# A decoder kernel: queries and keys projected once and turned by a shuffle, the cross attentions' sums taken two units to a step, the other products in the steps between, in halves of one bank

## The chip, the cores and the metric

The kernel runs on one core of a Trainium2 chip. The profile names the core's engines PE (the matrix engine; PEld is its weight load), DVE (the vector engine), ACT (the scalar engine), POOL, and SP, which issues transfers. The metric is the device time of one launch in microseconds (us): before the change the median of three runs is 1469.78 us (1468.67 to 1469.87).

## What is computed

The input is 16 batches of 128 tokens with 256 channels. Two decoder layers follow each other, each with self attention, cross attention and a feed-forward part, a residual sum and a layer norm after each. The two cross attentions matter here. In layer 0, which projects and rotates its queries and keys, the reference says (cut):

```python
q = jnp.einsum('oi,bit->bot', wq, x) + bq[None, :, None]
k = jnp.einsum('oi,bit->bot', wk, c) + bk[None, :, None]
v = jnp.einsum('oi,bit->bot', wv, c) + bv[None, :, None]
...
q = apply_rope(q, ROPE_D)
k = apply_rope(k, ROPE_D)
scores = jnp.einsum('bhqc,bhkc->bhqk', q, k) / math.sqrt(K_CHANNELS)
...
p_attn = jax.nn.softmax(scores, axis=-1)
out = jnp.einsum('bhqk,bhkc->bhqc', p_attn, v)
...
out = jnp.einsum('oi,bit->bot', wo, out) + bo[None, :, None]
```

It has 16 heads of 8 channels. The rotation multiplies each of a head's first four channels by a cosine and adds, times a sine, the channel two places away. Layer 1's cross attention has 8 heads of 16 channels and no projections: its queries are the tokens, its keys and values both the context.

## The kernel before

**Beats.** Each attention is written as a pipeline in beats. `by_beats` (L274) gets blocks of (beats per batch, lag, scores, jobs, order of batches). In every beat it first calls the scores' `beat(s, t)`, then `sums` if any are due, then the jobs that are due. PE runs its products in exactly this order (`mm`, L238, and `turned`, L242, keep it), and the attention's DVE, ACT and POOL instructions are kept in program order too (`Written`, L190). So an instruction that waits holds up everything behind it on its engine.

**Scores.** A unit is what one beat handles: two heads of one chunk of 128 queries or keys. `cross_scores` (L428) does two things in one beat. For the unit `s` it makes scores in a tile `ps_st` (two PSUM banks), whose negated row maxima DVE takes with a TENSOR_REDUCE. For the unit `t`, which is `lag` beats older, it makes the transposed scores less the maxima in another `ps_st`, from which ACT's exponential writes `pT`. Both use products on a quarter of PE's rows, so they run side by side; in the trace they are the groups of form 32*128. Late in the pipeline three `ps_st` tiles go round, so the scores of one beat go where the exponential of the beat before has read.

**Sums.** `sums` (L472) multiplies the exponentials with the values, in products of form 128*32, into `ps_o` (one bank). It is due two beats after its unit's exponential: one unit in each beat. In layer 0 a unit takes 8 matmul instructions, in layer 1 it takes 16 (an f32 product is two instructions in the trace).

**Jobs.** All other products of the two cross attentions go into `ps_m`. After a `switch` in the course of each pipeline it is one bank with one buffer. Each job sits at a beat offset from its batch's first beat. In layer 0 (8 beats per batch, lag 11, L975) the jobs with PE products are `keys` (-10), `queries` (-5), `values` (5), `maxima` (9), `finish` (26), `gate_turn` (28), and for every second batch `gate` (32) and `places` (39). Taken modulo 8 these fall on eight different beats. `queries` and `keys` call `side` (L920): two projections of 256 columns into one bank, the second with the weights' rows swapped so that it holds the mate channels; `rotated` (L800) then does cosine times the first on DVE, a bias on the second on ACT, sine times it and the sum on POOL. In layer 1 (4 beats per batch, lag 6, L1380) the jobs with products are `values` (0), `cross_maxima` (5), `turn_block` (18), and for every second batch `route` (19), `score` (23 and 24).

**What follows a job.** Each product in `ps_m` is read by ACT or DVE: `values` by an ACT copy to `v`, `maxima` by an ACT copy to `nmT` that the next exponentials' products need, `gate_turn` by an ACT copy. In both layers `out` copies `ps_o` on ACT, `invert` takes a logarithm and an exponential of the sums on ACT (`ol`), and the layer norm's `rstd` is a POOL instruction between DVE instructions.

Layer 0's feed-forward part (eight experts) and layer 1's (dense, plus a lookup) lie outside the attention pipelines and have their own loops.

Of the kernel before, what the change touches and what calls it, by code (L numbers as in the profile page):

```python
# [18 lines left out]
P = 128  # L19
D = 256  # L20
# [11 lines left out]
def kernel(ctx: ExitStack, tc: tile.TileContext, a: dict, out: bass.AP):  # L32
# [121 lines left out]

    xw = load(cpool, [P, 8, P], a["xw"], "xw", eng=nc.gpsimd)
    xb = load(cpool, [P, 6], a["xb"], "xb", eng=nc.gpsimd)
    bv2 = load(cpool, [P, D], a["bv2"].partition_broadcast(P), "bv2", eng=nc.gpsimd)
# [87 lines left out]
    class InTurn:  # L245
# [5 lines left out]
        def tile(self, *args, **kw):  # L251
            self.n += 1
            return self.pools[self.n % len(self.pools)].tile(*args, **kw)

    def attention_tiles(st, ahead):
# [4 lines left out]
        single = st.enter_context(tc.tile_pool(name="ps_m", bufs=1, space=PSUM))  # L260
        extra = st.enter_context(ExitStack())
        more = extra.enter_context(tc.tile_pool(name="ps_m2", bufs=2, space=PSUM))
        pl = dict(st=scores, o=sums, m=InTurn(more, single, more))

        def switch():
            extra.close()
            pl["st"] = InTurn(scores, scores, extra.enter_context(tc.tile_pool(name="ps_st2", bufs=1, space=PSUM)))
            pl["m"] = single

        for name, bufs in (("w", 2), ("q", ahead), ("p", 4)):  # L270
            pl[name] = st.enter_context(tc.tile_pool(name=f"att_{name}", bufs=bufs))
        return pl, switch

    def by_beats(blocks, switch=None, at=None):  # L274
# [153 lines left out]
    def cross_scores(pl, heads, kept, lag):  # L428
# [68 lines left out]

        return dict(beat=beat, sums=sums)

# [406 lines left out]
    def rope_cross_plain(pl):  # L906
# [4 lines left out]
        def biases(b):  # L911

            if b:
                return
            pb = pl["m"].tile([P, 1], F32, name="ps_m")
            mm(pb, lhsT=xw[:, 5, :], rhs=xb[:, 5:6], start=True, stop=True)
            bias_of["ov"] = const.tile([P, 1], F32, name="bias_ov")
            vec.tensor_tensor(bias_of["ov"], pb, xb[:, 4:5], ALU.add)

        def side(b, n, src):  # L920
            pab = pl["m"].tile([P, 2, D], F32, name="ps_m")
            for i in range(2):
                mm(pab[:, i, :], lhsT=xw[:, 2 * n + i, :], rhs=src, start=True, stop=True)
            return rotated(pl, pab, n, "wq"[n])

        def queries(b):
            q = side(b, 0, x_t[b])
            z = pl["q"].tile([P, 4, D], F32, name="z")
            for i in range(4):
                pool.tensor_scalar_mul(z[:, i, :], q, hm[:, 2 + i : 3 + i])  # L930
            kept[b]["qz"] = z

        def keys(b):
            kept[b] = {}
            kept[b]["k"] = side(b, 1, ctx_t[b])

        def values(b):
            pv = pl["m"].tile([P, 2, P], F32, name="ps_m")
            for kc in range(2):
                mm(pv[:, kc, :], lhsT=ctx_t[b][:, kc * P : (kc + 1) * P], rhs=xw[:, 4, :], start=True, stop=True)  # L940
            v = kept[b]["v"] = v8[b % 2]
# [25 lines left out]
        def finish(b):  # L967
            oT = kept[b][1]
            kept[b] = cross_output(pl, b, bias_of["ov"], (6, oT[:, 0, :]), (7, oT[:, 1, :]))
# [12 lines left out]
        return 8, 11, cross_scores(pl, 16, kept, 11), jobs, range(B)  # L982

    def rope_cross_masked(st):
# [3 lines left out]
        for b in range(B):  # L988
            rot = []
            for n, src in ((0, x_t[b]), (1, ctx_t[b])):  # L990
                pab = pl["m"].tile([P, 2, D], F32, name="ps_m")
                nc.tensor.matmul(pab[:, 0, :], lhsT=xw[:, 2 * n, :], rhs=src, start=True, stop=True)
                nc.tensor.matmul(pab[:, 1, :], lhsT=xw[:, 2 * n + 1, :], rhs=src, start=True, stop=True)
                rot.append(rotated(pl, pab, n, "w"))
            z = pl["w"].tile([P, 4, D], F32, name="z")
# [3 lines left out]
            for kc in range(2):  # L999
                nc.tensor.matmul(  # L1000
                    pv[:, kc, :], lhsT=ctx_t[b][:, kc * P : (kc + 1) * P], rhs=xw[:, 4, :], start=True, stop=True
                )
# [4 lines left out]
            oT = cross_heads(pl, 16, rot[0], [z[:, i, :] for i in range(4)], v, dict(masked, v=vn))  # L1007
            xn, stats = cross_output(pl, b, xb[:, 4:5], (5, oT.rearrange("p c q -> p (c q)")))
            scaled(x_t[b], xn, stats)
# [178 lines left out]
    with ExitStack() as st:  # L1188
# [177 lines left out]
        def best(b):  # L1366
# [10 lines left out]
            for hf in range(2):  # L1377
# [234 lines left out]
def layouts(inputs):  # L1612
# [6 lines left out]

    mate = row + np.where(c < 2, 2, np.where(c < 4, -2, 0))  # L1620
    theta = np.float32(1.0) / np.float32(10000.0) ** (np.arange(0, 4, 2, dtype=np.float32) / np.float32(4))
# [13 lines left out]
    for n in range(2):  # L1635
# [10 lines left out]
        "w0": np.stack([i[f"L0_attn_w_{n}"].T for n in "qkvo"], 1),  # L1646
        "xw": np.stack([wq.T, wq[mate].T, wk.T, wk[mate].T, wv.T, wo.T] + pairs, 1),
        "xb": np.stack([bq, bq[mate], bk, bk[mate], bo, i["L0_xattn_bv"]], 1),
        "bv2": np.concatenate([i["L0_xattn_bv"]] * 2),
# [43 lines left out]
```

## Time and profile before

| What | Value |
|---|---|
| Median of the runs | 1469.78 us |
| The profiled execution's own time | 1472.02 us |
| Its span, from first to last instruction | 1470.3 us |
| Mean granted clock of PE | 0.959 |
| DVE busy | 810.8 us |
| ACT busy | 595.7 us |
| POOL busy | 289.6 us |
| DVE's row maxima (TENSOR_REDUCE on `ps_st`) | 256 of 1221 ns |
| ACT's exponentials (`pT`) | 224 of 1024 ns |

The stretches of the span, by the view of windows (busy us of each engine):

| Stretch (us) | Work | PE | DVE | ACT | clock |
|---|---|---|---|---|---|
| 35 to 200 | layer 0 self attention, cross attention filling | 151.42 | 148.53 | 75.37 | 0.99 |
| 200 to 500 | layer 0 cross attention | 298.76 | 228.00 | 173.37 | 0.99 |
| 500 to 860 | end of it, experts, start of layer 1 | 304.72 | 59.37 | 71.14 | 0.90 |
| 860 to 1020 | layer 1 self attention | 158.60 | 122.23 | 76.34 | 0.96 |
| 1020 to 1210 | layer 1 cross attention | 175.37 | 125.86 | 108.01 | 0.99 |
| 1210 to 1470 | layer 1 feed-forward | 237.88 | 104.69 | 88.00 | 0.96 |

A row of the timeline gives start, length, engine, line, operation, output<-inputs, shapes and how many were merged; in brackets stands how long the engine had been idle and what ended that. A line of the view of windows gives the stretch, its length, each engine's busy time with the count of instructions, and PEclk, the share of full speed that PE's clock was granted.

### The profile page before, as it was taken

What the parts mean: (1) busy time and instruction counts of PE and PEld (TensorE: products, weight loads), DVE (VectorE), ACT (ScalarE), POOL (GpSimd) and SP (SyncE); (2) the same over time, 40 slices, a digit from 0 to 9 for tenths busy, and PEclk for the clock granted to TensorE, in tenths of its full rate; (3) what the DMA queues carried; (4) which work ended last, traced back from release to release, by engine and by line L of the source; (5) the groups of instructions that cost most, each with busy time, mean ns of one, the idle gap of its engine ahead of it and who ended that gap; (6) DMA issues with size and microseconds to landing.
All of it is one profiled execution on the core that took longest, in us unless ns stands there. A gap on an engine that the chain in (4) does not pass through costs nothing. (4 is left out here: it accounts for less than half of the span.)

```text
span 1470.3 us, 28836 instructions
## 1 busy us (share of the span) xinstructions
PE 1338.7 (91%) x11993; PEld 857.1 (58%) x11993; DVE 810.8 (55%) x2085; ACT 595.7 (41%) x1051; POOL 289.6 (20%) x402
## 2 busy tenths in 40 slices
PE   3999999999999938999999589999999989989997
PEld 2656555555555415777888456665555544446666
DVE  6899876777777530100110168876767656543222
ACT  1454426555655611111112135543555556761110
POOL 7000243344444120000000233312121100000000
PEclk9999989999999968999999769999999998999999
DMA  9200000000000006222330411000000000000000
GB/s 300 68 2 2 2 1 2 2 16 16 16 12 12 23 28 193 96 94 92 112 129 15 158 37 31 23 2 1 2 1 2 2 2 1 0 2 15 15 8 22
DMA packets 42780, 57.15 MB, mean 39 GB/s; under 512 B 5929, under 2 KB 32569, under 8 KB 42633
## 3 DMA queue, kind: packets, MB, share of 16 engines
q1 hardware_dynamic: 37192, 41.99, 8.8%
q0 software_dynamic: 4608, 12.34, 2.6%
q8 instruction: 99, 1.62, 0.5%
q10 hardware_dynamic: 832, 0.80, 0.2%
q14 instruction: 49, 0.39, 0.1%
HBM read 38.73 MB, written 16.38 MB: 37 GB/s over the span
## 5 line engine op out<-in xcount | busy, mean ns | idle before, releaser
L199 DVE TENSOR_REDUCE nm<-ps_st 128x4 f32<-128x1024 f32 (+1 forms) x256 | 312.6, 1221 | 123.1 <-PE ps_st L240 119.7
L199 ACT ACTIVATE pT<-ps_st 128x1024 f32<-128x1024 f32 x224 | 229.4, 1024 | 197.3 <-PE ps_st L240 195.5
L199 POOL TENSOR_TENSOR rstd<-ve,nhalf 128x1 f32<-128x1 f32 x112 | 62.7, 561 | 752.1 <-DVE ve L199 630.9
L240 PE MATMUL ps_o<-pT,v 128*32 128x256 f32 (+1 forms) x2560 | 164.5, 347 | 0.5 <-DVE oT L199 0.4
L240 PE MATMUL ps_st<-rot,z 32*128 32x256 f32 x1024 | 147.8, 405 | 2.2 <-DVE nm L199 2.2
L1077 DVE TENSOR_TENSOR ye<-ps_e,b 128x256 f32<-128x256 f32 (+6 forms) x38 | 16.1, 424 | 238.7 <-PE ps_e L1074 238.7
L240 PE MATMUL ps_st<-z,rot 32*128 32x512 f32 x512 | 131.7, 592 | 0.0
L1066 ACT ACTIVATE h<-ps_h,b 128x672 f32<-128x672 f32 (+7 forms) x64 | 46.6, 728 | 204.3 <-PE ps_h L1062 192.3
L1062 PE MATMUL ps_h<-h,w 128*128 128x336 f32 (+7 forms) x512 | 122.1, 399 | 0.0
L1062 PEld LDWEIGHTS ps_h<-h,w 128*128 128x128 f32 x512 | 97.2, 190 | 23.6
L240 PEld LDWEIGHTS ps_o<-pT,v 128*32 128x32 f32 x2560 | 54.6, 108 | 96.2 <-issue 82.4
L240 PE MATMUL ps_st<-nmT,pick 32*128 32x256 bf16 x1024 | 100.7, 274 | 9.8 <-ACT nmT L199 7.4
L240 PEld LDWEIGHTS ps_st<-rot,z 32*128 32x128 f32 x1024 | 91.0, 187 | 14.5 <-issue 5.1
L199 POOL DMA_INDIRECT y<-ys,place x32 | 31.1, 973 | 284.6 <-DVE absT L1195 276.9
L240 PE MATMUL ps_o<-pT,ones 128*32 128x256 f32 x1024 | 79.2, 380 | 0.0
L240 PEld LDWEIGHTS <-pick 32*128 32x128 bf16 x1024 | 30.3, 92 | 79.1 <-issue 72.1
L240 PE MATMUL ps_st<-ctx,z 32*128 32x256 f32 x512 | 73.1, 403 | 0.0
L240 PE MATMUL ps_f<-fxT,fgw 128*128 128x512 f32 x128 | 62.4, 611 | 7.1 <-ACT g L1409 7.1
L1062 PE MATMUL ps_h<-xeT,w 128*128 128x336 f32 (+7 forms) x256 | 65.2, 414 | 4.0 <-DVE xeT L1054 2.1
L1074 PE MATMUL ps_e<-w,h 128*128 128x256 f32 (+6 forms) x304 | 67.3, 379 | 0.0
L240 PE MATMUL ps_st<-z,ctx 32*128 32x512 f32 x256 | 66.6, 596 | 0.0
L1074 PEld LDWEIGHTS ps_e<-w,h 128*128 128x128 f32 (+6 forms) x304 | 54.9, 181 | 11.0 <-issue 1.0
(295 smaller groups left out, 2356.2 us busy)
## 6 DMA issues: line engine op xcount, KB each, us to landing
w<-in_W_dram SPq DMA_DIRECT2D x16, 512.0 KB, 4.0
w<-in_W_dram SPq DMA_DIRECT2D x8, 1024.0 KB, 5.7
xs<-zero SPq DMA_DIRECT2D x42, 128.0 KB, 4.2
xe<-xs SPq DMA_DIRECT2D x32, 128.0 KB, 3.5
ys<-ye SPq DMA_DIRECT2D x32, 128.0 KB, 3.7
x<-in_x_dram SPq DMA_DIRECT2D x16, 128.0 KB, 7.4
ctx<-in_ctx_dram POOLq DMA_DIRECT2D x16, 128.0 KB, 5.9
out_dram<-x SPq DMA_DIRECT2D x16, 128.0 KB, 1.7
```

Source lines behind the costliest of these rows:

```text
L199: instruction = getattr(self.engine, name)(*args, **kw)
L240: tc.keep_in_program_order(nc.tensor.matmul(*args, **kw))
L1062: nc.tensor.matmul(ps[:, n, 0:H], lhsT=w[:, c, hc * P : (hc + 1) * P], rhs=src[:, c, n * H : (n + 1) * H], start=(c == 0), stop=(c == part ...
L1066: nc.scalar.activation(dst[:, hc, 0:cap].rearrange("p (n t) -> p n t", n=2), ps[:, :, 0:H], AF.Gelu, bias=b12[:, layer, hc : hc + 1],)
L1074: nc.tensor.matmul(ps[0:m], lhsT=h2[:, fc, c : c + m], rhs=w3[:, fc, :], start=(fc == 0), stop=(fc == 3))
L1077: nc.vector.tensor_add(ye[0:m, c // P, :], ps[0:m], b3[0:m])
```

## The change

**Sums in pairs.** `cross_scores` returns `pairs=True`, and `by_beats` puts an odd unit's sums one beat earlier, so that two units' sums stand in one beat and the next beat has none. This holds for both cross attentions.

**Jobs between.** The offsets of the jobs move so that those with PE products mostly fall on the beats without sums. Layer 0's lag becomes 12. Layer 0's PE jobs are now `keys` -11, `queries` -7, `values` 7, `maxima` 10, `finish` 27, `gate_turn` 29, `gate` 33, `places` 39. In layer 1 `values` is at -1, `turn_block` at 17; `cross_out`, `cross_invert` and `cross_add` are one beat earlier than before.

**One projection, and a shuffle.** `side` goes. `projected` makes one projection and ACT adds its bias (`plain`). A beat later `rotated` shuffles `plain` across partitions on DVE to get the mate channels and multiplies by the cosine on DVE; sine and sum stay on POOL. The swapped weights and biases leave the inputs. The masking of the queries by head (`one_head_left`, four POOL instructions) becomes a job of its own.

**Half banks.** After the switch `ps_m` is one tile of a whole bank, `ps_half`, and jobs take its two halves in turn (`Halves`). Before the switch the three banks that were two pools become one pool of three.

```diff
+    class Halves:
+        def __init__(self, bank):
+            self.bank, self.n = bank, 0
+
+        def tile(self, shape, dtype, name):
+            self.n += 1
+            half = self.bank[:, self.n % 2, :]
...
         def switch():
             extra.close()
             pl["st"] = InTurn(scores, scores, extra.enter_context(tc.tile_pool(name="ps_st2", bufs=1, space=PSUM)))
-            pl["m"] = single
+            last = extra.enter_context(tc.tile_pool(name="ps_m2", bufs=1, space=PSUM))
+            pl["m"] = Halves(last.tile([P, 2, D], F32, name="ps_half"))
...
-                    beats.setdefault(n + lag + 2, [[], [], []])[1].append((score["sums"], b, h))
+                    late = h % 2 if score.get("pairs") else 0
+                    beats.setdefault(n + lag + 2 - late, [[], [], []])[1].append((score["sums"], b, h))
...
-    def rotated(pl, pab, n, dst):
-
+    def biased(pl, ps, n):
+
+        t = pl["w"].tile([P, D], F32, name=f"plain{n}")
+        act.activation(t, ps, AF.Identity, bias=xb[:, n : n + 1])
+        return t
+
+    def rotated(pl, plain, n, dst):
+
+        t1 = pl["w"].tile([P, D], F32, name="rot_t")
+        vec.stream_shuffle(t1, plain, mates)
         t0 = pl[dst].tile([P, D], F32, name=f"rot{n}")
-        t1 = pl["w"].tile([P, D], F32, name="rot_t")
-        vec.scalar_tensor_tensor(t0, pab[:, 0, :], xb[:, 2 * n : 2 * n + 1], rope[:, 0, :], ALU.add, ALU.mult)
-        act.activation(t1, pab[:, 1, :], AF.Identity, bias=xb[:, 2 * n + 1 : 2 * n + 2])
+        vec.tensor_tensor(t0, plain, rope[:, 0, :], ALU.mult)
         pool.tensor_tensor(t1, t1, rope[:, 1, :], ALU.mult)
         pool.tensor_tensor(t0, t0, t1, ALU.add)
         return t0
...
-        def side(b, n, src):
-            pab = pl["m"].tile([P, 2, D], F32, name="ps_m")
-            for i in range(2):
-                mm(pab[:, i, :], lhsT=xw[:, 2 * n + i, :], rhs=src, start=True, stop=True)
-            return rotated(pl, pab, n, "wq"[n])
+        def projected(n, src):
+            pq = pl["m"].tile([P, D], F32, name="ps_m")
+            mm(pq, lhsT=xw[:, n, :], rhs=src, start=True, stop=True)
+            return biased(pl, pq, n)
...
-        jobs = [(8, parts), (9, maxima), (20, out), (21, spread), (22, invert), (25, divide), (-11, biases), (-10, keys),
-                (-5, queries), (5, values), (26, finish), (27, scale_rows)]
-        for beat, part in ((28, gate_turn), (32, gate), (33, gate_best), (35, gate_rows), (39, places)):
+        jobs = [(8, parts), (10, maxima), (20, out), (21, spread), (22, invert), (24, divide), (-12, biases), (-11, keys),
+                (-10, turn_keys), (-7, queries), (-6, turn_queries), (-5, one_head_left), (7, values), (27, finish),
+                (28, scale_rows)]
+        for beat, part in ((29, gate_turn), (33, gate), (34, gate_best), (36, gate_rows), (39, places)):
...
-        return 8, 11, cross_scores(pl, 16, kept, 11), jobs, range(B)
+        return 8, 12, cross_scores(pl, 16, kept, 12), jobs, range(B)
...
-            [(4, cross_parts), (5, cross_maxima), (11, cross_out), (12, cross_invert), (13, cross_add), (14, cross_scale),
-             (0, values), (-2, queries), (18, turn_block), (19, route), (23, lambda b: score(0, b)),
+            [(4, cross_parts), (5, cross_maxima), (10, cross_out), (11, cross_invert), (12, cross_add), (14, cross_scale),
+             (-1, values), (-2, queries), (17, turn_block), (19, route), (23, lambda b: score(0, b)),
```

More of the change, by code (lines that the diff above doesn't have):

```diff
@@ L152 @@
     nc.gpsimd.memset(zero, 0.0)
-    xw = load(cpool, [P, 8, P], a["xw"], "xw", eng=nc.gpsimd)
-    xb = load(cpool, [P, 6], a["xb"], "xb", eng=nc.gpsimd)
+    xw = load(cpool, [P, 6, P], a["xw"], "xw", eng=nc.gpsimd)
+    xb = load(cpool, [P, 4], a["xb"], "xb", eng=nc.gpsimd)
     bv2 = load(cpool, [P, D], a["bv2"].partition_broadcast(P), "bv2", eng=nc.gpsimd)
@@ L253, in tile @@
             return self.pools[self.n % len(self.pools)].tile(*args, **kw)
+    class Halves:
[4 more added lines that the diff above has]
+            half = self.bank[:, self.n % 2, :]
+            if dtype == BF16:
+                half = half.bitcast(BF16)
+            half = half[0 : shape[0], 0 : math.prod(shape[1:])]
+            return half if len(shape) == 2 else half.rearrange("p (a b) -> p a b", a=shape[1])
     def attention_tiles(st, ahead):
@@ L259, in attention_tiles @@
         sums = st.enter_context(tc.tile_pool(name="ps_o", bufs=1, space=PSUM))
-        single = st.enter_context(tc.tile_pool(name="ps_m", bufs=1, space=PSUM))
         extra = st.enter_context(ExitStack())
-        more = extra.enter_context(tc.tile_pool(name="ps_m2", bufs=2, space=PSUM))
-        pl = dict(st=scores, o=sums, m=InTurn(more, single, more))
+        pl = dict(st=scores, o=sums, m=extra.enter_context(tc.tile_pool(name="ps_m", bufs=3, space=PSUM)))
         def switch():
@@ L496, in sums @@
                 )
-        return dict(beat=beat, sums=sums)
+        return dict(beat=beat, sums=sums, pairs=True)
     def attention_pools(st):
@@ L797, in ternary @@
         return 2, 3, causal_scores(pl, kept, qk_scale), jobs, range(B)
-    def rotated(pl, pab, n, dst):
+    mates = [n + (2 if n % 8 < 2 else -2 if n % 8 < 4 else 0) for n in range(32)]
+    def biased(pl, ps, n):
[5 more added lines that the diff above has]
+        vec.stream_shuffle(t1, plain, mates)
         t0 = pl[dst].tile([P, D], F32, name=f"rot{n}")
-        t1 = pl["w"].tile([P, D], F32, name="rot_t")
-        vec.scalar_tensor_tensor(t0, pab[:, 0, :], xb[:, 2 * n : 2 * n + 1], rope[:, 0, :], ALU.add, ALU.mult)
-        act.activation(t1, pab[:, 1, :], AF.Identity, bias=xb[:, 2 * n + 1 : 2 * n + 2])
+        vec.tensor_tensor(t0, plain, rope[:, 0, :], ALU.mult)
         pool.tensor_tensor(t1, t1, rope[:, 1, :], ALU.mult)
@@ L915, in biases, with turn_queries, one_head_left, turn_keys @@
             pb = pl["m"].tile([P, 1], F32, name="ps_m")
-            mm(pb, lhsT=xw[:, 5, :], rhs=xb[:, 5:6], start=True, stop=True)
+            mm(pb, lhsT=xw[:, 3, :], rhs=xb[:, 3:4], start=True, stop=True)
             bias_of["ov"] = const.tile([P, 1], F32, name="bias_ov")
-            vec.tensor_tensor(bias_of["ov"], pb, xb[:, 4:5], ALU.add)
-        def side(b, n, src):
-            pab = pl["m"].tile([P, 2, D], F32, name="ps_m")
-            for i in range(2):
-                mm(pab[:, i, :], lhsT=xw[:, 2 * n + i, :], rhs=src, start=True, stop=True)
-            return rotated(pl, pab, n, "wq"[n])
+            vec.tensor_tensor(bias_of["ov"], pb, xb[:, 2:3], ALU.add)
+        def projected(n, src):
+            pq = pl["m"].tile([P, D], F32, name="ps_m")
+            mm(pq, lhsT=xw[:, n, :], rhs=src, start=True, stop=True)
+            return biased(pl, pq, n)
         def queries(b):
-            q = side(b, 0, x_t[b])
+            kept[b]["q"] = projected(0, x_t[b])
+        def turn_queries(b):
+            kept[b]["q"] = rotated(pl, kept[b]["q"], 0, "w")
+        def one_head_left(b):
             z = pl["q"].tile([P, 4, D], F32, name="z")
             for i in range(4):
-                pool.tensor_scalar_mul(z[:, i, :], q, hm[:, 2 + i : 3 + i])
+                pool.tensor_scalar_mul(z[:, i, :], kept[b]["q"], hm[:, 2 + i : 3 + i])
             kept[b]["qz"] = z
         def keys(b):
-            kept[b] = {}
-            kept[b]["k"] = side(b, 1, ctx_t[b])
+            kept[b] = {"k": projected(1, ctx_t[b])}
+        def turn_keys(b):
+            kept[b]["k"] = rotated(pl, kept[b]["k"], 1, "q")
         def values(b):
@@ L939, in values @@
             for kc in range(2):
-                mm(pv[:, kc, :], lhsT=ctx_t[b][:, kc * P : (kc + 1) * P], rhs=xw[:, 4, :], start=True, stop=True)
+                mm(pv[:, kc, :], lhsT=ctx_t[b][:, kc * P : (kc + 1) * P], rhs=xw[:, 2, :], start=True, stop=True)
             v = kept[b]["v"] = v8[b % 2]
@@ L968, in finish @@
             oT = kept[b][1]
-            kept[b] = cross_output(pl, b, bias_of["ov"], (6, oT[:, 0, :]), (7, oT[:, 1, :]))
+            kept[b] = cross_output(pl, b, bias_of["ov"], (4, oT[:, 0, :]), (5, oT[:, 1, :]))
         def scale_rows(b):
@@ L990, in rope_cross_masked @@
             for n, src in ((0, x_t[b]), (1, ctx_t[b])):
[L991 to L994, printed above, removed]
+                pq = pl["m"].tile([P, D], F32, name="ps_m")
+                nc.tensor.matmul(pq, lhsT=xw[:, n, :], rhs=src, start=True, stop=True)
+                rot.append(rotated(pl, biased(pl, pq, n), n, "w"))
             z = pl["w"].tile([P, 4, D], F32, name="z")
@@ L1000, in rope_cross_masked @@
                 nc.tensor.matmul(
-                    pv[:, kc, :], lhsT=ctx_t[b][:, kc * P : (kc + 1) * P], rhs=xw[:, 4, :], start=True, stop=True
+                    pv[:, kc, :], lhsT=ctx_t[b][:, kc * P : (kc + 1) * P], rhs=xw[:, 2, :], start=True, stop=True
                 )
@@ L1007, in rope_cross_masked @@
             oT = cross_heads(pl, 16, rot[0], [z[:, i, :] for i in range(4)], v, dict(masked, v=vn))
-            xn, stats = cross_output(pl, b, xb[:, 4:5], (5, oT.rearrange("p c q -> p (c q)")))
+            xn, stats = cross_output(pl, b, xb[:, 2:3], (3, oT.rearrange("p c q -> p (c q)")))
             scaled(x_t[b], xn, stats)
@@ L1618, in layouts @@
     c = row % 8
-    mate = row + np.where(c < 2, 2, np.where(c < 4, -2, 0))
     theta = np.float32(1.0) / np.float32(10000.0) ** (np.arange(0, 4, 2, dtype=np.float32) / np.float32(4))
@@ L1646, in layouts @@
         "w0": np.stack([i[f"L0_attn_w_{n}"].T for n in "qkvo"], 1),
-        "xw": np.stack([wq.T, wq[mate].T, wk.T, wk[mate].T, wv.T, wo.T] + pairs, 1),
-        "xb": np.stack([bq, bq[mate], bk, bk[mate], bo, i["L0_xattn_bv"]], 1),
+        "xw": np.stack([wq.T, wk.T, wv.T, wo.T] + pairs, 1),
+        "xb": np.stack([bq, bk, bo, i["L0_xattn_bv"]], 1),
         "bv2": np.concatenate([i["L0_xattn_bv"]] * 2),
```

## The prediction, made before the changed kernel ran

> **What bounds the kernel now.** I read the page first, then the windows (PE is busy for 298.76 of 300 us from 200 to 500), then the timeline beat by beat.
>
> ```profile
> PE 1338.7 (91%) x11993; PEld 857.1 (58%) x11993; DVE 810.8 (55%) x2085; ACT 595.7 (41%) x1051; POOL 289.6 (20%) x402
> ```
>
> PE sets the pace, but "busy" hides two waits of PE on ACT. The first stands inside a beat's score group. Layer 0, PE, then ACT:
>
> ```profile
> 217.15 0.39 PE L240 MATMUL ps_st<-nmT,pick 32*128 32x256 bf16 x4
> 217.38 1.02 PE L240 MATMUL ps_st<-z,rot 32*128 32x512 f32 x4
> 217.92 1.13 PE L240 MATMUL ps_st<-rot,z 32*128 32x256 f32 x8
> 218.99 0.64 PE L240 MATMUL ps_o<-pT,v 128*32 128x256 f32 x8
> 219.56 0.28 PE L240 MATMUL ps_st<-nmT,pick 32*128 32x256 bf16 x2
> 219.59 0.48 PE L240 MATMUL ps_st<-rot,z 32*128 32x256 f32 x2
> ```
>
> ```profile
> 216.76 1.02 ACT L199 ACTIVATE pT<-ps_st 128x1024 f32<-128x1024 f32 x1
> 218.51 1.02 ACT L199 ACTIVATE pT<-ps_st 128x1024 f32<-128x1024 f32 x1 [0.73 <-PE ps_st L240]
> ```
>
> The beat from 217.15 starts its scores (rot,z) only at 217.92, just after the exponential of the beat before (216.76 + 1.02 = 217.78) frees the tile: its score group takes 1.84 (to 218.99). The beat from 219.56 need not wait: 1.18 (to 220.74). The exponential starts 1.36 after its beat, so (*) **score group = the larger of 1.18 and 3.59 - the length of the beat before** (1.75 there: 1.84). Sums of one unit take 0.57 (218.99 to 219.56).
>
> The second wait stands between two jobs of one beat. Layer 1, the beat from 1080.56, PE, then ACT:
>
> ```profile
> 1081.74 0.64 PE L240 MATMUL ps_o<-pT,v 128*32 128x256 f32 x8
> 1082.19 0.61 PE L240 MATMUL ps_o<-pT,ones 128*32 128x256 f32 x8
> 1082.74 0.44 PE L243 MATMUL ps_m<-ident,ctx 128*128 128x128 f32 x2
> 1083.95 0.66 PE L240 MATMUL ps_m<-fkeys,fq_T 64*128 64x64 f32 x4 [0.77 <-ACT v L199]
> 1084.54 0.28 PE L240 MATMUL ps_st<-nmT,pick 32*128 32x256 bf16 x2
> ```
>
> ```profile
> 1081.86 1.02 ACT L199 ACTIVATE pT<-ps_st 128x1024 f32<-128x1024 f32 x1 [0.93 <-PE ps_st L240]
> 1082.78 0.86 ACT L199 ACTIVATE ol<-ol 128x256 f32<-128x256 f32 x2
> 1083.54 0.35 ACT L199 COPY v<-ps_m 128x256 f32<-128x256 f32 x1
> ```
>
> `values` and `score` share the bank. The second must wait until ACT has read the first, and ACT first does the exponential, then logarithm and exponential. The second job starts 3.39 after its beat. PE idles only 0.77 of that, because 1.00 of sums (16 instructions) lies in front.
>
> **What the change removes.** One projection per side: two f32 instructions. From sums of 8 instructions (0.57) and of 16 (1.00), four cost 0.215, so `queries` falls from 1.06 (305.50 to 306.56) to 0.64, `keys` likewise: 0.85 a batch. Joining two units' sums saves 0.14 a pair (0.57 + 0.57 to 1.00). Jobs that share a beat share one group's overhead, about 0.2.
>
> **What it moves (the core).** ACT reads the first job late, so the second's start is fixed by ACT's queue. The built order of the changed kernel names each instruction's wait: the second product of a beat, though in the other half of `ps_half`, waits for the ACT copy of the first. The Trainium skill, "PSUM — Partial Sum Buffer" (section on bank collisions), says "Semaphore-guard PSUM by **bank × quadrant** (by bank is the simple version), not by address": it speaks against halves as buffers. By it, and by the 0.77 row (one bank before too), I price a wait; with free halves the sum would be that of rival B.
>
> Layer 0, beats of one batch, by (*), (s) marking sums: 0(s) 1.18 + 1.00; 1 `queries` 0.64; 2(s) with `maxima` 1.22; 3 `finish` 1.06; 4(s); 5 `keys`, then `gate_turn`; 6(s); 7 `values` 0.64. In 5 the bias copy ends at 1.36 + 1.02 + 0.47 + gaps = 2.9, then `gate_turn` 0.37: 3.29. Every second batch `gate` waits in 1 (2.92 + 0.99 = 3.91) and `places` in 7 (3.11). Lengths: 2.18, 2.05, 2.76, 2.24, 2.35, 3.29, 2.18, 2.05 = 19.10, and 2.54, 3.91, 2.40, 2.25, 2.34, 3.29, 2.18, 3.11 = 22.02; mean 20.56. The same recurrence for the kernel before (1.75 plus jobs 0.22, 1.06, 1.06, 0.37, 0.64, 1.06, with `gate` 0.99 and `places` 0.19 in every second batch) gives 20.3; the trace has 87 beats in 220 us, 20.2. So +0.27 x 14.5 batches = **+4**: the savings are eaten.
>
> Layer 1: 0(s) 1.18 + 1.86 = 3.04, plus `score` 0.59 in half: 3.34. 1: `maxima` ends at 1.46, `nmT` at 1.30 + 1.02 + 0.37 = 2.70, then `turn_block` 0.37: 3.13 (before 2.93, with the wait for `nmT` under the sums). 2(s): 3.04. 3: `values`, then ACT as in the rows above (`invert` moved along into this beat): second job at 3.39, `score` 0.59 or `route` 1.09: mean 4.23. Sum 13.74; before, two batches take 23.55 (1060.99 to 1084.54), 11.78 each. The sums no longer lie under ACT's queue. +1.96 x the 10 batches with such a third beat, + 1.2 x three earlier ones = **+23**.
>
> **Clock.** Windows of 3.41 us:
>
> ```profile
> 156.00:159.40 3.40, 2.19 (x44) 1.42 (x39) 2.54 (x6) 1.85 (x4) 1.41 (x3) 1.00 0.00 0
> 193.50:196.90 3.40, 1.99 (x18) 1.07 (x14) 3.26 (x8) 0.69 (x2) 0.14 (x1) 1.00 0.00 0
> 196.90:200.30 3.40, 3.00 (x14) 1.89 (x16) 3.26 (x9) 0.61 (x3) 1.31 (x2) 0.50 0.00 0
> 1022.90:1026.30 3.40, 1.81 (x18) 1.20 (x16) 2.58 (x5) 2.03 (x2) 3.05 (x4) 1.00 0.00 0
> 1026.30:1029.70 3.40, 3.38 (x28) 1.90 (x31) 1.39 (x2) 1.02 (x1) 1.15 (x2) 0.51 0.00 0
> ```
>
> PE busy for 2.19 keeps the clock; 1.99 or 1.81 is followed by half clock. The Trainium skill's "TensorE: Matmul & The Clock Gate" (Part 1) lets the clock fall after an idle window of about 3.4 us, and asks only for no gap over that: by it the stalls here cost nothing more. But the gaps at 1022.90 were 0.85 and 0.76 (PE's timeline); the row decides. Layer 1's third beat leaves PE idle from 1.62 to 3.39, 1.77. A window falls if it holds over some 1.37 of that, so at 72% of placements: 7 of 10. A window at half clock loses at most 1.7; I take 1.5: **+10**. From below nothing, from above 17 (every batch). Layer 0's stall of about 1.1 leaves 2.3 busy: no fall.
>
> **Smaller parts.** The shuffle of 256 columns is not in the trace; between the 256-wide TENSOR_TENSOR (0.42) and the 512-wide shuffle (0.73) I take 0.45, as the 512-wide pair is 0.73 to 0.68. Per side DVE gains 0.45 + 0.42 - 0.48 = 0.39. In the joint stretch DVE has slack (161.16 of 210 us): hidden; uncovered, 32 x 0.39 = 12. In the filling DVE is full (3.26 of 3.40 at 193.50): five sides, **+2**. One more beat of lag turns one joint beat (2.5) into a scores-only (1.7) and an exponential-only one (1.75): within that +2's error. `rstd` now stands on POOL behind four maskings (4 x 0.93); DVE's normalisation behind it, and the next row maxima, come about 0.9 late. They are needed two beats later, and `gate_turn` waits for its bias copy longer: hidden; each us over that costs 16. The loads shrink, before PE starts. Three-buffer `ps_m` before the switch is as before. Layer 0's end chain and the experts stay.
>
> **Sum.** 4 + 23 + 10 + 2 = +39 on a span of 1470.3. The profiled execution took 1472.02, the runs' median is 1469.78; a difference carries over, so 1469.8 + 39 = **1509**.
>
> **Rivals.**
> A. As summed: 1509. Chance 0.5.
> C. The stalls come, the clock holds: 1499. 0.28.
> D. Layer 0's stalls also drop the clock (2.3 against the 2.19 that held), or DVE's additions show: 16 x 1.5 on top, about 1533. 0.1.
> B. The halves work as two buffers. Then beat 5 of layer 0 takes 2.09 and the recurrence gives 18.7 a batch (-1.6 x 14.5 = -23); layer 1 gives 11.5 (-4): about 1445. It decides from the point where the second job does not wait. The half-size jobs and joined sums speak for it, the built waits against it. 0.04.
> E. Layer 1's second jobs wait less than the queue shows, under half, and layer 0's savings stand: about 1475. 0.08, half of it within or under no change.
>
> Range 1484 to 1532: C and A with their bounds. A difference under 0.2% (3 us) can't be told from none. Faster 0.06, within 0.02, slower 0.92.
>
> **What would show it.** In layer 1, `fkeys` or `fxT,fq` idle 1.7 "<-ACT v", and `ident,x` idle about 1.3 "<-ACT nmT" in every batch; in layer 0 `ident,x` idle about 1.1 behind ACT `plain`; the stretch from `ps_st<-ctx,z` on over 20 us longer; PEclk 0.5 in several windows there. Wrong, if those brackets are missing or layer 0's batches take under 19.5.

## The result, and the profile after

The changed kernel takes **1496.75 us** (median of four runs, 1495.77 to 1497.36) against 1469.70 for the kernel before in the same comparison. The ratio is 1.0185, with a 95% interval of 1.0172 to 1.0199: slower by 27 us. The profiled execution has a span of 1494.9 us and a mean clock of 0.953. First the page's line of busy times, the answer to the one that opened the prediction:

```profile
PE 1322.5 (88%) x11929; PEld 857.3 (57%) x11929; DVE 813.3 (54%) x2149; ACT 593.9 (40%) x1051; POOL 291.2 (19%) x402
```

PE has 16 us less to do, and its share of the span has fallen: what was saved has become waiting, and more waiting has come. The groups of PE in layer 1's joint stretch (1045 to 1207; after the last bar the idle time in front of the group and what ended it):

```profile
L240 PE MATMUL ps_half<-fkeys,fq_T 64*128 64x64 f32 x40 | 6.6, 284 | 8.8 <-ACT v L199 8.8
L240 PE MATMUL ps_half<-fxT,fq 128*128 128x128 f32 x40 | 6.0, 293 | 8.9 <-ACT v L199 8.9
L243 PE MATMUL ps_half<-ident,x 128*128 128x128 f32 x24 | 5.2, 300 | 14.1 <-ACT nmT L199 14.1
```

The kernel before, in its own joint stretch (1045 to 1202), has the same two waits, but smaller:

```profile
L240 PE MATMUL ps_st<-nmT,pick 32*128 32x256 bf16 x220 | 21.5, 272 | 6.0 <-ACT nmT L199 6.0
L240 PE MATMUL ps_m<-fkeys,fq_T 64*128 64x64 f32 x48 | 7.9, 284 | 3.9 <-ACT v L199 3.9
```

These are thirteen of 0.46 and five of 0.77. In the changed kernel, ten stalls behind `v` make 17.7 us, 1.77 each (five stand before `fxT,fq`, five before a first `fkeys,fq_T`), and twelve behind `nmT` make 14.1, 1.17 each. Both can be seen being made in the timeline, PE and then ACT:

```profile
1080.94 0.28 PE L243 MATMUL ps_half<-identb,nmx 128*128 128x128 bf16 x2
1082.40 0.44 PE L243 MATMUL ps_half<-ident,x 128*128 128x128 f32 x2 [1.17 <-ACT nmT L199]
...
1087.00 0.44 PE L243 MATMUL ps_half<-ident,ctx 128*128 128x128 f32 x2
1089.20 0.66 PE L240 MATMUL ps_half<-fkeys,fq_T 64*128 64x64 f32 x4 [1.77 <-ACT v L199]
```

```profile
1087.12 1.02 ACT L199 ACTIVATE pT<-ps_st 128x1024 f32<-128x1024 f32 x1 [0.58 <-PE ps_st L240]
1088.04 0.85 ACT L199 ACTIVATE ol<-ol 128x256 f32<-128x256 f32 x2
1088.80 0.35 ACT L199 COPY v<-ps_half 128x256 f32<-128x256 f32 x1
```

`values` is done at 1087.44. ACT still has the beat's exponential in hand, then the logarithm and exponential, and only then copies `v`. Nothing stands in front of the second product: in the kernel before, 1.00 us of sums lay there.

In layer 0 (235 to 450) the same kind of row:

```profile
L240 PE MATMUL ps_half<-wg,gate_xT 128*128 128x8 f32 x40 | 5.3, 259 | 4.3 <-ACT plain L199 4.3
L243 PE MATMUL ps_half<-ident,x 128*128 128x128 f32 x20 | 4.4, 301 | 8.8 <-ACT plain L199 7.9 <-DVE oh L199 0.9
```

**Where the time came from.** ACT's exponentials are counted off in the trace and their starts compared; this leaves out the start of the launch, where the first exponential came between 40.4 and 44.6 us in the profiled executions of this study, whatever the kernel.

| From which to which exponential | Work | Before (us) | Changed (us) | Difference |
|---|---|---|---|---|
| 24 to 48 | filling of layer 0's cross attention | 94.02 | 98.48 | +4.46 |
| 48 to 144 | layer 0's joint stretch, 12 batches | 243.11 | 242.66 | -0.45 |
| 144 to 160 | its end, the experts, start of layer 1 | 385.12 | 382.98 | -2.14 |
| 160 to 192 | layer 1's self attention | 149.71 | 149.30 | -0.41 |
| 192 to 255 | layer 1's cross attention | 179.11 | 204.02 | +24.91 |

Layer 1's cross attention is nearly the whole loss. In layer 0 the saved projections have brought nothing that can be seen.

PE's clock plays into these lengths. It is granted in full or at half, and the half comes in pieces of 3.41 us, called windows here. One costs about 1.6 us where PE sets the pace: layer 1's cross attention, put back as before, takes 177.49 us in a trace with no half-clock window in it (`l0_spread` below) and 179.07 in one with one (`l1_restored`). In the table, layer 1's row has one window before and two after, so that 23.3 of the 24.9 us are not the clock's. Layer 0's second row has none before and two after.

### The profile page after: what moved, and what is told of

It reads as the page before. It is cut to its first block, busy times and chain, and to the rows that moved or that the text cites. A ratio compares the mean times of both kernels' runs of the same rounds, so it can differ in the third digit from the quotient of the medians.

```text
span 1494.9 us, 28761 instructions
## 1 busy us (share of the span) xinstructions
PE 1322.5 (88%) x11929; PEld 857.3 (57%) x11929; DVE 813.3 (54%) x2149; ACT 593.9 (40%) x1051; POOL 291.2 (19%) x402
## 5 line engine op out<-in xcount | busy, mean ns | idle before, releaser
L240 PE MATMUL ps_o<-pT,v 128*32 128x256 f32 (+1 forms) x2560 | 155.6, 349 | 1.8 <-ACT pT L199 1.3
L240 PE MATMUL ps_st<-rot,z 32*128 32x256 f32 x1024 | 152.8, 417 | 2.0 <-DVE nm L199 1.8
L240 PEld LDWEIGHTS ps_o<-pT,v 128*32 128x32 f32 x2560 | 65.5, 110 | 76.6 <-issue 49.0
```

The source lines that it names most:

```text
L240: tc.keep_in_program_order(nc.tensor.matmul(*args, **kw))
```

## The experiments

The median of the kernel before, run beside them, lay between 1470.09 and 1473.00 in these comparisons, so the ratio is the safer number. "Layer 1's stretch" is the last row of the table above, "layer 0's" its second.

### Layer 1: which part costs?

**Layer 1 put back.**

```diff
-            4, 6, cross_scores(pl, 8, kept1, 6),
-            [... (10, cross_out), (11, cross_invert), (12, cross_add), ... (-1, values), ... (17, turn_block), ...]
+            4, 6, cross_scores(pl, 8, kept1, 6, pairs=False),
+            [... (11, cross_out), (12, cross_invert), (13, cross_add), ... (0, values), ... (18, turn_block), ...]
```

> The changed kernel with layer 1's cross attention put back (its own offsets, sums of one unit a beat); layer 0 as changed. Theory (layer 1's waits are the loss, +24.6 of the stage times): 1472 us, layer 1 back at 11.8 us a batch. Rival (the loss lies in layer 0 or in the clock, and the stage times only show it late): 1480 or more.

Measured: 1470.08 us, ratio 0.9998 (0.9985 to 1.0010). Layer 1's stretch takes 179.07 us, as before. The loss is layer 1's; what the change does in layer 0, filling included, is worth nothing in sum.

**The old offsets, the sums still joined.**

```diff
-            [... (10, cross_out), (11, cross_invert), (12, cross_add), ... (-1, values), ... (17, turn_block), ...]
+            [... (11, cross_out), (12, cross_invert), (13, cross_add), ... (0, values), ... (18, turn_block), ...]
```

> The changed kernel with layer 1's jobs at the offsets of before, but the sums still two units in a step. Theory (joined sums and shared beats hurt together: each alone leaves the wait under something): the beat rule gives 12.3 us a batch against 13.6, so 1496.8 - 1.3 x 13 = 1480 us, with no idle over 1 us behind ACT v. Rival 1 (the joining is the loss): 1495. Rival 2 (the moved jobs are the loss): 1472.

Measured: 1491.39 us, ratio 1.0137 (1.0107 to 1.0168), near the first rival's number. In its groups (1045 to 1201) the wait for `v` is small, 2.3 us, but another product now stands behind `nmT`:

```profile
L240 PE MATMUL ps_st<-nmT,pick 32*128 32x256 bf16 x200 | 19.6, 272 | 15.2 <-ACT nmT L199 15.2
L240 PE MATMUL ps_half<-fkeys,fq_T 64*128 64x64 f32 x40 | 6.6, 284 | 2.3 <-ACT v L199 2.3
```

15.2 over 13 batches are again 1.17. The beat of the maxima holds no sums now, so PE comes to the next beat's first product, which needs `nmT`, before ACT has copied it. No shared bank is needed for this stall. The beat rule had said 12.3 us a batch and two batches without a clock loss took 24.76, 12.38 each. Where the forecast of the time failed is the rest: layer 1's stretch is 11.2 us shorter than in the changed kernel (192.85), not 17, since the changed kernel's first batches, which have no `route` or `score`, were shorter than 13.6; the stretch from exponential 144 to 160 is 3.8 longer, and the first exponential came 3.0 later, so the profiled execution kept only part.

**The sums single again, `values` and `turn_block` still early.**

```diff
-            4, 6, cross_scores(pl, 8, kept1, 6),
-            [... (10, cross_out), (11, cross_invert), (12, cross_add), ...]
+            4, 6, cross_scores(pl, 8, kept1, 6, pairs=False),
+            [... (11, cross_out), (12, cross_invert), (13, cross_add), ...]
```

> The changed kernel with layer 1's sums one unit a beat again, but values and turn_block still one beat earlier, in the beats that they share with route or score and with the maxima. Theory (joined sums and shared beats hurt together): sums of 1.00 us lie under ACT's queue again, the beat rule gives 12.0 us a batch, so 1496.8 - 1.6 x 13 = 1476 us, idle behind ACT v about 0.8. Rival 1 (the joining is the loss): 1472. Rival 2 (the moved jobs are the loss): 1495.

Measured: 1473.50 us, ratio 1.0031 (1.0018 to 1.0044). The same two waits are there (1045 to 1187), but cut down by the sums in front of them:

```profile
L240 PE MATMUL ps_half<-fkeys,fq_T 64*128 64x64 f32 x40 | 6.6, 284 | 3.1 <-ACT v L199 3.1
L240 PE MATMUL ps_half<-fxT,fq 128*128 128x128 f32 x40 | 5.8, 288 | 3.1 <-ACT v L199 3.1
L243 PE MATMUL ps_half<-ident,x 128*128 128x128 f32 x24 | 5.2, 300 | 5.6 <-ACT nmT L199 5.6
```

0.62 for 1.77, and 0.47 for 1.17. In layer 1's stretch, then, the joining alone adds 13.7 us (192.85 less 179.11), the moves alone 2.0 (181.14), both 24.9: 9.1 come only when both are there. The four traces have two, no, two and (before) one half-clock windows in it; with these taken out at 1.6 each, the three differences are 12.1, 3.6 and 23.3. PE's waits in the same stretch, in us:

| Layer 1's jobs | Sums | behind `v` | behind `nmT` |
|---|---|---|---|
| at the old beats | single (before) | 3.9 | 6.9 |
| at the old beats | joined | 2.3 | 17.6 |
| moved | single | 6.1 | 6.9 |
| moved | joined (changed) | 17.7 | 17.6 |

The longer wait for `nmT` comes from the joining alone. The long wait for `v` needs both: the moves put a second product behind `values` in ten batches in place of five, and the joining takes away the sums in front of it. My theory that neither does much without the other holds for `v` and fell for the whole; the joining is the main cause.

**Is it ACT's queue?** `values` listed ahead of `cross_invert`, so that ACT copies `v` first:

```diff
-            [(4, cross_parts), ... (11, cross_invert), ... (-1, values), (-2, queries), ...]
+            [(-1, values), (4, cross_parts), ... (11, cross_invert), ... (-2, queries), ...]
```

> The changed kernel with layer 1's values listed ahead of cross_invert in their common beat, so that ACT copies the values before it takes logarithm and exponential (0.86 us). Theory (the second product of that beat waits for ACT's queue): idle behind ACT v falls from 1.77 to 0.9, a batch of layer 1 from 13.63 to 12.8, 12 to 13 batches: 1486 us. Rival (the wait is something else, a fixed price of the bank): idle stays 1.77, 1497 us.

Measured: 1492.13 us, ratio 1.0144 (1.0122 to 1.0166). The stall fell as expected; in the groups of PE from 1040 to 1200:

```profile
L240 PE MATMUL ps_half<-fxT,fq 128*128 128x128 f32 x48 | 7.0, 288 | 5.1 <-ACT v L199 5.1
L240 PE MATMUL ps_half<-fkeys,fq_T 64*128 64x64 f32 x40 | 6.6, 284 | 5.1 <-ACT v L199 5.1
```

These are five stalls in each row, of 1.02 in place of 1.77, so PE waits 7.5 us less. Between the exponentials 200 and 248 (12 batches) the kernel is 9.1 us shorter (151.74 against 160.81); the changed kernel has one half-clock window there and this one none, which leaves 7.5 for the stalls. The profiled execution took 1487.05, close to the forecast, and the median of four runs keeps less of it. So the order of ACT's work makes 0.75 of each 1.77; the size in the whole is uncertain by some us.

**Do the halves do anything?** One plain tile in place of two halves:

```diff
-            last = extra.enter_context(tc.tile_pool(name="ps_m2", bufs=1, space=PSUM))
-            pl["m"] = Halves(last.tile([P, 2, D], F32, name="ps_half"))
+            pl["m"] = extra.enter_context(tc.tile_pool(name="ps_m2", bufs=1, space=PSUM))
```

> The changed kernel with one plain tile of the last bank in place of its two halves. Theory (the halves never work as two buffers, since each product waits for the reader of the one before it in either half): no change, 1497 us, the same idle of 1.77 behind ACT v. Rival (the halves save some of the waits): 1502 or more.

Measured: 1498.79 us, ratio 1.0180 (1.0159 to 1.0201), as the changed kernel's 1.0185. The stalls are the same (1050 to 1214):

```profile
L240 PE MATMUL ps_m<-fxT,fq 128*128 128x128 f32 x40 | 6.7, 318 | 8.8 <-ACT v L199 8.8
L240 PE MATMUL ps_m<-fkeys,fq_T 64*128 64x64 f32 x40 | 6.6, 284 | 8.9 <-ACT v L199 8.9
```

As built, with the waits by bank that the Trainium skill asks for in "PSUM — Partial Sum Buffer" (section on bank collisions), the two halves are one buffer. Whether two halves could overlap without those waits was not tried.

### The clock

**A longer batch.** Each pair of `turn_block`'s transposes is done three times, the same values written again:

```diff
-            for c in range(2):
+            for c in (0, 1, 0, 1, 0, 1):
                 turned(ps[:, c, :], x_t[b][:, c * P : (c + 1) * P], ident)
```

> The changed kernel with each pair of layer 1's turn_block transposes done three times (the same values written again), so that a batch is about 0.35 us longer and no longer four clock windows long. Theory (the clock held because the stall of 1.77 us came at the same place of every fourth 3.41 us window): 0.35 x 13 = 4.5 us of work, and 3 to 7 windows of half clock in layer 1's joint stretch in place of one, 1.3 us each: 1505 to 1510 us. Rival (the clock holds through such stalls wherever they fall): 1501 us and at most one such window.

Measured: 1508.15 us, ratio 1.0247 (1.0228 to 1.0266). The forecast time is met, but not for its reason. The group of maxima and transposes grew from 1.83 to 2.26, so 12 batches have 5.2 us more work, where 0.35 a batch (4.2) had been taken. Between the exponentials 200 and 248 the clock fell in two windows: one more than in the changed kernel, fewer than the theory's three, more than the rival's one. Two windows of its joint stretch, each with the next (the view of windows: after the length PE, PEld, DVE, ACT and POOL busy, then PEclk):

```profile
1105.30:1108.70 3.40, 1.64 (x18) 1.51 (x22) 0.98 (x1) 2.04 (x5) 0.00 (x0) 1.00 0.03 5
1108.70:1112.10 3.40, 3.40 (x58) 1.86 (x50) 2.39 (x8) 1.02 (x1) 0.00 (x0) 1.00 0.01 2
1119.00:1122.40 3.40, 1.63 (x20) 1.30 (x22) 1.23 (x1) 2.27 (x5) 0.00 (x0) 1.00 0.02 5
1122.40:1125.80 3.40, 3.40 (x32) 1.21 (x30) 2.20 (x7) 1.02 (x1) 0.00 (x0) 0.50 0.00 0
```

PE is busy for 1.64 and for 1.63 of 3.40 us, and only the second is followed by half clock. So neither the theory nor the rival holds as put, and PE's busy time does not decide a fall. What differs is which products fill the busy part: in both windows PE stands 1.77 us behind `v`, but in the first (1105.3 to 1108.7) the products behind this wait fill PE's 128 rows, in the second (1119 to 1122.4) 64 of them.

```profile
L240 PE MATMUL ps_half<-fxT,fq 128*128 128x128 f32 x8 | 1.2, 288 | 1.8 <-ACT v L199 1.8
```

```profile
L240 PE MATMUL ps_half<-fkeys,fq_T 64*128 64x64 f32 x4 | 0.7, 284 | 1.8 <-ACT v L199 1.8
```

The last section counts this over all windows.

### Layer 0: where did the saving go?

**Every product in a beat of its own**, on top of layer 1 put back:

```diff
-        for beat, part in ((29, gate_turn), (33, gate), (34, gate_best), (36, gate_rows), (39, places)):
+        for beat, part in ((30, gate_turn), (36, gate), (37, gate_best), (38, gate_rows), (40, places)):
...
-            jobs.append((41 + 2 * k, ...
+            jobs.append((42 + 2 * k, ...
```

> Layer 1 put back as in the first kernel of this set, and in layer 0 gate_turn, gate and places moved to beats that hold no other product of the shared bank (30, 36, 40). Theory (in layer 0 the waits at the shared bank ate what the single projection and the joined sums saved): the beat rule gives 19.55 us a batch against 20.2 measured, so 9 to 15 us below the first kernel: about 1460 us. Rival (a second product in a beat costs layer 0 nothing, ACT or the exponentials bound it): the same as the first kernel, 1472.

Measured: 1469.82 us, ratio 0.9998 (0.9989 to 1.0007). The expected gain did not come: layer 0's stretch takes 240.06 us, 20.0 a batch, not 19.55. Something else had taken the place of the waits at the bank. Timeline of this kernel, POOL and then DVE:

```profile
365.74 3.63 POOL L199 TENSOR_SCALAR z<-rot,hm 128x256 f32<-128x256 f32 x4
369.34 0.57 POOL L199 TENSOR_TENSOR rstd<-ve,nhalf 128x1 f32<-128x1 f32 x1
```

```profile
369.94 0.41 DVE L199 TENSOR_SCALAR x<-xn,mv,rstd 128x256 f32<-128x256 f32 x1 [1.44 <-POOL rstd L199]
370.27 0.17 DVE L199 TENSOR_TENSOR gw<-ps_half,bg 128x16 f32<-128x16 f32 x1
370.47 0.17 DVE L199 TENSOR_REDUCE gm<-gw 128x2 f32<-128x16 f32 x1
```

`rstd`'s input is ready at 367.37 (`ve`), but POOL does the four maskings first. DVE stands 1.44 us at the layer norm, behind it the gate's maximum `gm` is late, and behind `gm` ACT's small exponentials, and behind these the exponential of the beat, which frees the tile for PE:

```profile
370.68 0.30 ACT L199 ACTIVATE gw<-gw,gm 128x8 f32<-128x8 f32 x1 [1.98 <-DVE gm L199]
371.26 1.00 ACT L199 ACTIVATE pT<-ps_st 128x1024 f32<-128x1024 f32 x1
```

This wait of DVE is there in the changed kernel too, and the spread jobs made it longer: `l1_restored` first, then this kernel, both from 260 to 480.

```profile
L199 DVE TENSOR_SCALAR x<-xn,mv,rstd 128x256 f32<-128x256 f32 x11 | 4.8, 438 | 12.2 <-POOL rstd L199 12.2
```

```profile
L199 DVE TENSOR_SCALAR x<-xn,mv,rstd 128x256 f32<-128x256 f32 x11 | 4.8, 439 | 22.6 <-POOL rstd L199 22.6
```

**`rstd` ahead of the maskings**, added to that:

```diff
-                (-10, turn_keys), (-7, queries), (-6, turn_queries), (-5, one_head_left), (7, values), (27, finish),
-                (28, scale_rows)]
+                (-10, turn_keys), (-7, queries), (-6, turn_queries), (27, finish), (-5, one_head_left), (7, values),
+                (28, scale_rows)]
```

> The kernel l0_spread (layer 1 as before, layer 0's products of the shared bank in beats of their own) with finish ahead of the four maskings on POOL, so that rstd does not wait behind them. In l0_spread DVE stands idle 1.4 us before x<-xn, behind it the row maxima of gate come late, and behind those ACT's exponential of the beat. Theory (with the waits at the bank gone, this wait sets layer 0's pace): that idle falls under 0.4, two batches take 39.5 in place of 40.5 us, 1463 us. Rival (something else bounds layer 0 at 20.2 us a batch): no change, 1470 us.

Measured: 1461.20 us, ratio 0.9930 (0.9910 to 0.9950). Layer 0's stretch takes 231.92 us, 19.33 a batch. DVE's wait is gone (250 to 480):

```profile
L199 DVE TENSOR_SCALAR x<-xn,mv,rstd 128x256 f32<-128x256 f32 x12 | 4.8, 404 | 0.0
```

**The same move without the spread jobs**, that is, the line above alone with layer 1 put back.

> Layer 1 as before, layer 0 as changed, and only finish ahead of the four maskings on POOL. DVE's idle before x<-xn behind POOL rstd (11.5 us over ten batches in the changed kernel) should go. Theory (in the changed kernel this lateness is hidden under the waits at the shared bank, and decides only once those are gone): 1470 us, as with layer 1 put back alone. Rival (rstd behind the maskings was layer 0's loss by itself): 1461 us.

Measured: 1470.21 us, ratio 0.9979 (0.9964 to 0.9994). Layer 0's stretch is 242.17 us against 242.67 without the move. So in that stretch the two moves alone are worth 0.5 (`rstd`) and 2.6 us (the spread beats), both together 10.8 (242.67 to 231.92). But two windows of half clock, some 1.6 us each, fell in each stretch of 242 us and none in the two shorter ones. Without them the spread beats alone gave nothing, and both together some 7.5. Two waits stood side by side in layer 0, and each covered for the other.

**The sums of layer 0 single again**, in the kernel with both moves:

```diff
-        return 8, 12, cross_scores(pl, 16, kept, 12), jobs, range(B)
+        return 8, 12, cross_scores(pl, 16, kept, 12, pairs=False), jobs, range(B)
...
-        jobs = [... (20, out), (21, spread), (22, invert), (24, divide), ...]
+        jobs = [... (21, out), (22, spread), (23, invert), (24, divide), ...]
```

> The kernel l0_spread_rstd with layer 0's sums one unit a beat again (out, spread and invert one beat later for it). Theory (in layer 0 the joined sums save 0.14 a pair and give most of it back to shorter beats between, whose successors wait for the exponential): the beat rule gives 19.79 against 19.55 us a batch, so +3.4: 1465 us. Rival 1 (joining costs layer 0 time, as it does layer 1): 1455. Rival 2 (the saving of 0.14 x 8 a batch is kept whole): 1477.

Measured: 1466.79 us, ratio 0.9964 (0.9953 to 0.9974); layer 0's stretch 234.14 us, 2.2 more (2.9 by the rule for 12 batches). In layer 0 joining does pay, a little.

**One projection and the shuffle without the moves:** layer 1 put back, layer 0 with lag 11, single sums and the jobs' beats of before, where no beat holds two of them. The turns and the maskings stay jobs of their own, a beat behind their projections, and the halves stay.

```diff
-        jobs = [(8, parts), (10, maxima), ..., (-11, keys), (-10, turn_keys), (-7, queries), (-6, turn_queries), ...]
+        jobs = [(8, parts), (9, maxima), ..., (-10, keys), (-9, turn_keys), (-5, queries), (-4, turn_queries), ...]
...
-        return 8, 12, cross_scores(pl, 16, kept, 12), jobs, range(B)
+        return 8, 11, cross_scores(pl, 16, kept, 11, pairs=False), jobs, range(B)
```

> The single projection with the shuffle alone: the changed kernel with layer 1 as before, and in layer 0 the beats, lag and single-unit sums of the kernel before, where no beat holds two products of the shared bank (only turn_keys, turn_queries and the maskings stand one beat after their products). Theory (the projection's saving of 0.85 a batch is real where nothing has to share a beat): the beat rule gives 19.46 us a batch against 20.29, 12 us less, of which the filling takes back about 4: 1462 us. Rival (the shuffle's added 0.39 us of DVE a side comes to light in the joint stretch): 1470 us or more.

Measured: 1464.19 us, ratio 0.9938 (0.9915 to 0.9961). The time was met, its parts were not: layer 0's stretch saves only 2.8 us (240.29), and the filling is 1.6 shorter, not 4 longer. In the joint stretch DVE's added work does come to light, as the rival said, for example in PE's timeline:

```profile
338.53 0.28 PE L243 MATMUL ps_half<-identb,nmx 128*128 128x128 bf16 x2 [1.50 <-DVE nmx L199]
```

There a shuffle stands in DVE's queue ahead of the eight small operations of `places`, and the row maxima behind both.

### A version ahead of both

The kernel with both moves in layer 0, and layer 1's `values` listed ahead of `cross_invert` (offset 0, as before the change):

> The kernel l0_spread_rstd with layer 1's values listed ahead of cross_invert, in the beat where both stand as in the kernel before. Theory (the idle of 0.77 before fkeys in every second batch of layer 1 is ACT's logarithm and exponential ahead of the copy of the values): it goes, 6 x 0.77 = 4.6 us: 1457 us. Rival (later logarithm and exponential hold up cross_add and what hangs on it): 1461 us or more.

Measured: **1459.23 us**, ratio 0.9901 (0.9868 to 0.9935). Between the exponentials 200 and 248 it takes 136.60 us where the kernel without it takes 138.14: 1.5 us, not 4.6. The wait for `v` did not go: PE stands behind it five times for 0.46 in place of 0.77 (2.3 us for 3.9). ACT is now ready before the product is, and what is left is mainly the copy itself, 0.37; 5 x 0.31 is this 1.5. The kernel with layer 0's two moves alone has 0.9930, and the intervals overlap; only that both beat the kernel before is shown.

## Why the prediction was right in its direction and 12 us too high

In sum, of the forecast +39 the profiled executions show 24.6 (the runs' medians 27): in layer 1 +24.9 for +23 and +10, in layer 0 -0.5 for +4, in the filling +4.5 for +2, and -4.4 in the rest, for which nothing had been taken. Half of that rest, -2.1, lies from exponential 144 to 160, where the changed kernel spent one window less at half clock.

**Layer 1, +23.** Right in mechanism and size. Two batches take 27.26 us (1103.96 to 1131.22), 13.63 each where 13.74 was worked out; the stretch grew by 24.9, of which 1.6 is the clock's. The forecast stalls are 1.77 (1.7 forecast) and 1.17 (about 1.3). The runs add which part matters: the joining alone is 13.7 of it. One reading was not right: before, the wait for `nmT` did not lie wholly under the sums, PE stood 0.46 there in each batch.

**Clock, +10: the term that was mis-sized.** The step was "A window falls if it holds over some 1.37 of that, so at 72% of placements: 7 of 10". In that joint stretch one window fell. A run of the same work with one plain tile shows three, and one with longer batches two. The cost of a window was about right (1.5 taken): that one-tile kernel has three more half-clock windows in layer 1's stretch than the changed one and takes 4.7 us more, 1.6 each. So the term came to 1.6 us in place of 10. Two things were wrong in the count. The limit drawn from single rows of PE's busy time, busy for 2.19 keeps the clock and 1.99 loses it, does not hold (1.64 kept it above, and in layer 0 2.54, from 279.6 to 283.0, lost it). And placements were taken as independent, while two batches are 27.26 us, 7.99 windows of 3.41: the stalls keep their place against the windows, and after the first one lay whole in a window, the others lay across a border. In the changed kernel, first a stall inside a window and what followed it, then a later one:

```profile
1071.50:1074.90 3.40, 1.63 (x15) 1.06 (x10) 1.22 (x1) 2.00 (x4) 0.00 (x0) 1.00 0.00 0
1074.90:1078.30 3.40, 3.40 (x27) 1.86 (x29) 0.53 (x1) 1.00 (x2) 0.00 (x0) 0.50 0.00 0
1085.10:1088.50 3.40, 2.33 (x34) 1.15 (x26) 1.83 (x3) 1.94 (x4) 0.00 (x0) 1.00 0.00 0
```

How many fall hangs on where the windows lie against the stalls. Counted by the bound of the last section, with the windows shifted over the changed kernel's trace in 40 even steps, between 1 and 10 of them would fall in this stretch, 5.9 in the mean: 7 was not far from the mean. This is rough, as every fall shifts what follows, and how launches differ in it was not studied; the four runs lie within 1.6 us of one another. So the rival in which the clock holds, 1499, came nearest. The Trainium skill's "TensorE: Matmul & The Clock Gate" (Part 1), by its rule that only a gap of some 3.4 us lowers the clock, would have put this term at nothing and been nearer here, though the row above shows a fall with no gap over 1.77. The same part also tells of a kernel whose clock swings because PE idles briefly between groups, which fits this row, but gives no size for it.

**Layer 0, +4.** It came out at -0.45 for 12 batches (+3.2 of the +4 was meant for them), with two windows of half clock in it, where the prediction had none. Without these, at 1.6 each, it is some -3.7: the waits ate less of the savings than was priced, and it is luck that the clock brought the number nearer to the forecast. Two batches without one take 40.27 us (41.12 worked out): the three beats with a second product measured 3.20, 3.73 and 2.90 where 3.29, 3.91 and 3.11 were taken, since small gaps that I had added between ACT's instructions are not there. That waits eat most of the savings was right; that the waits at the bank are what eats them was half of it.

**`rstd` behind the maskings, hidden.** True for the kernel as changed (the move alone is worth 0.5 us in layer 0's stretch), and wrong as soon as the bank's waits go: then it is worth 8.1 (240.06 to 231.92). "Hidden" should have named the cover, the wait at the bank, as the thing that an improvement would take away.

**Filling, +2.** It took +4.5. Between the exponentials 24 and 32 it is 2.7, about DVE's share as forecast (its 256-wide shuffle takes 0.437 us, 0.45 was assumed). The rest comes while the clock is at half, for 10.2 us in the kernel before (first row) and 23.9 in the changed one (second), and the prediction had put that at nothing; the last section counts why it stays:

```profile
196.90:207.10 10.20, 9.80 (x42) 5.79 (x42) 7.65 (x17) 1.71 (x4) 1.88 (x3) 0.50 0.00 0
```

```profile
194.20:218.10 23.90, 23.26 (x116) 12.49 (x118) 16.58 (x37) 5.26 (x10) 7.94 (x11) 0.50 0.00 1
```

**Rivals.** Halves as two buffers (1445) is refuted by the plain tile. Stalls under half in layer 1 (1475) is refuted by the rows of 1.77. A clock loss in every batch of layer 0 (1533) did not come, though two windows fell there (283.0 and 405.9), each after one with PE busy for 2.54, against "no fall".

## What to carry to other kernels

Work that stands in front of a wait is its cover: before joining or moving it, look at which engine's answer the next instruction needs, and when that answer comes; sums of 1.00 us were cheap because 1 us of waiting lay under them. When a saving disappears, look for two waits side by side, and take both away in one run: here 0.5 us and nothing alone were some 7.5 together in one stretch, with the clock's share taken out. In an in-order queue the place of a 0.6 us instruction (`rstd`) or of a copy (`v`) may cost more than a projection (8.1 us over 12 batches, 0.68 each, against 0.43), and moving it ahead cost nothing that shows in these runs.

## What the hardware showed that I had not expected

Half clock came in pieces of 3.41 us or multiples of it, and PE's busy time tells neither its beginning nor its end. At PE busy for 23.26 of 23.9 us it did not lift, while before the change it lifted after 10.2. Windows with PE busy for 1.64 us kept the clock and one with 2.24 lost it:

```profile
190.80:194.20 3.40, 2.24 (x18) 1.48 (x16) 3.33 (x7) 0.31 (x1) 1.30 (x2) 1.00 0.00 0
```

Another count does separate them: how much of the matrix engine the products fill. Take each product's columns, times the share of the 128 rows and of the 128 columns that its form names (256 columns of form 32*128 count as 256 x 32/128), and twice for f32 (512 f32 columns take 429 ns from start to start, 512 bf16 columns 216). A window filled throughout holds some 8100 of these, by the same times. All fourteen traces, cut at the borders of their half-clock pieces from 40 us on, give:

| Clock in the window, then in the next | Windows | Filled columns |
|---|---|---|
| full, then half | 96 | at most 3028 |
| full, then full | 5125 | at least 3031, but for one with 2839 |
| half, then half | 424 | at most 3061 |
| half, then full | 96 | at least 3089 |

So in these traces the clock falls after a window filled to under some 37%, and lifts after one filled to more than about that. The two windows of the longer batch hold 3047 (kept) and 1999 (lost). The 23.9 us are seven windows; six hold 1368 to 2852, and only the last, 3653, is over the bound: scores on a quarter of the rows keep PE busy and fill little. The count was chosen after the runs, to fit them; no run was made to test it.

The stretch from exponential 144 to 160, with nearly the same instructions in every kernel, took 381.4 to 386.8 us in this study's traces: up to 384.3 where the clock was at half for 82 us of it, and from 384.8 on where it was at half for 85 to 92. Single runs of one kernel spread over up to 10.5 us. Stage lengths from the trace, with their half-clock windows counted, told changes apart that the runs' medians could not.
